# Attention's PSUM copies issued one slot later, and a respaced softplus, in a state-space, attention and graph-experts kernel

## The chip, the cores and the metric

The kernel runs on one core of one Trainium2 chip. The metric is device time in microseconds (us) from start to end of one execution; for the kernel before it is the median of three runs. Beside these there is one profiled execution, from which every busy time, wait and instruction duration below is taken.

## The reference, cut to what matters

Layer 0 is a group norm and two selective state-space passes ("t" along the 96 steps of each sequence, "d" along the 32 variables). Layer 1 is additive attention over 3072 tokens of each of 4 batches, then a graph attention that gates four experts. The change touches the step size of the state-space pass and the attention.

```python
# layer 0, both passes
xc = silu(conv1d(x @ in_w_x) + conv_b)
dt, Bm, Cm = split(xc @ xproj_w)
dt = softplus(dt @ dt_w + dt_b)                 # the softplus that the change respaces
h  = exp(dt * A) * h + dt * Bm * xc             # scan over the sequence, 16 states
y  = (sum_s(h * Cm) + xc * D) * silu(z)
x  = x + y @ out_w
# layer 1, attention, t = tokens of a batch
q, k = t @ Wt, t @ Wx
e = tanh(q[:, None, :] + k[None, :, :] + bh) @ Wa + ba
t = t + softmax(e) @ t                          # values: the normalized tokens
# then the graph attention, the gates and the experts (gelu)
```

## The kernel before, in words

**Order.** ScalarE (ACT), VectorE (DVE), TensorE (PE) and GpSimd (POOL) run in the order in which the program issues. It is written out by hand as slots. `Attention.units` and layer 0's `run` are two generators that are advanced in turn. A slot is: attention's tanh; the first half of layer 0's jobs (decay exponentials and scans); attention's score products; the second half of layer 0's jobs (the front of the next block, inputs, outputs, gates, side products of experts); attention's next small step from the list `todo`; one step of side work (`beside`: keys, or the table of a finished part). DMAs are issued from SP.

**Layer 0.** A block is 384 tokens and takes 48 slots, in which four chunks of 128 channels pass through 16 states. In every three slots `back` computes four decays dA (`decays`, exponential on ScalarE into one of two PSUM banks), and scans them on VectorE a slot later (`scans`, L395). GpSimd multiplies and sums (L402 to L411). Beside it `front` prepares the next block: the convolution, and from slot 31 the step sizes. `step` makes one chunk's softplus as max(s, 0) + log(1 + u) with u = exp(-|s|): a product pt into the PSUM bank "pp" (one buffer, shared with px, pd, pz and po); on VectorE max (L300) and -|s| (L301); on ScalarE u (L308); on GpSimd 1+u (L312); on VectorE (1+u)-1-u (L316), a rounding remainder that GpSimd subtracts from dt (L320). One logarithm over all four chunks (L329) and two additions (L335) end it. Blocks called `lead`, whose fronts run before attention begins, use other engines for some of these.

**Attention.** One tanh (L802) of 128 x 3072 elements serves four query rows. Its output th has three buffers. Two slots later 16 products (`scores`, L778) fold it into the PSUM tile pe (one buffer). Eight slots make a unit of 32 rows; at its end `unit_tail` takes the negated row maximum nb on VectorE (L848) and the exponential pr on ScalarE (L855). Then come, one per slot from `todo`: `turn` of four pieces (transposes, L862, and their copy pT, L864), `turn` of two, `values` (48 products, L871), `kept` (copy pvs, L877). Four units make a tile, whose tail goes on: `factors` (L900 to L907), `factors2` (L912, L914), `factors3` (exponential), `spread` (GpSimd, L921), `together` (L926), `outputs` (L934 to L937). If steps are left when the next unit ends, they are all issued at once, ahead of the new exponential. All these products, and the side work's, use one PSUM bank ("pv").

**Late part.** When layer 0 has ended, the first half of each slot is edge-sorting work on VectorE, paced by an estimate of 1.9 us, and the second half early expert products, paced by `att.extra`, the estimated TensorE time of the next step.

What a step looked like: the products and the copy that reads them stand together.

```python
for i in range(i0, i1):
    nc.tensor.transpose(pt[:, (i - i0) * P:(i - i0 + 1) * P], pr[:, i * P:(i + 1) * P], self.ident)
nc.vector.tensor_copy(pT[:, i0:i1, :].rearrange("p i x -> p (i x)"), pt[:, :(i1 - i0) * P])
```

Of the kernel before, what the change touches and what calls it, by code (L numbers as in the profile page):

```python
# [26 lines left out]
P = 128  # L27
# [47 lines left out]
class Layer0:  # L75
# [96 lines left out]
    def front(self, blk, lead):  # L172
# [107 lines left out]
        def step(e, s_mm, s_out):  # L280
# [22 lines left out]
            @at(s_out + 1)  # L303
            def _():
                if lead:
                    nc.scalar.activation(ua(), ua(), AF.Exp, scale=-1.0)
                else:
                    nc.scalar.activation(ua(), ua(), AF.Exp, bias=self.wf["dtb"][:, e:e + 1])  # L308

            @at(s_out + 2)  # L310
            def _():
                nc.gpsimd.tensor_scalar(ub(), ua(), 1.0, None, ALU.add)  # L312

            @at(s_out + 3)
            def _():
                nc.vector.scalar_tensor_tensor(ua(), ub(), 1.0, ua(), ALU.subtract, ALU.subtract)  # L316

            @at(s_out + 5)
            def _():
                nc.gpsimd.tensor_tensor(dt(), dt(), ua(), ALU.subtract)  # L320

        step(0, 33, 33)
        step(1, 34, 35)
        step(2, 36, 36)
        step(3, 37, 37)

        @at(41)
        def _():
            nc.scalar.activation(v["ub"], v["ub"], AF.Ln)  # L329

        for e in range(0, EC, 2):
            @at(44 + e // 2)
            def _(e=e):
                dt = blk["dt"][:, e:e + 2, :]
                nc.vector.tensor_tensor(dt, dt, v["ub"][:, e:e + 2, :], ALU.add)  # L335
# [11 lines left out]
    def back(self, blk, then):  # L347
# [121 lines left out]
        for e in range(EC):  # L469
# [18 lines left out]
            put(12 * e + 1, skip(e))  # L488
            put(12 * e + 4, gate_product(e), 0 if blk["lead"] else 1)
            put(12 * e + 5, gate_tanh(e))  # L490
            put(12 * e + 6, gate_out(e))
            if blk["lead"]:
# [139 lines left out]
class Attention:  # L632
# [4 lines left out]
    def __init__(self, ctx, tc, ident, a, x1, x2, xn2T, tab_s, tab_a):  # L637
# [34 lines left out]
        self.extra, self.entry, self.col, self.asked, self.normed = 0.0, 0, 0, 0, 0  # L672

    def psum(self, name):
        return self.ps_v.tile([P, JB], F32, tag="pv", name=name)
# [90 lines left out]
    def units(self, side):  # L766
# [23 lines left out]
        i = 0  # L790
        while i < B * PER + LAG or todo:
            b, col = self.entry, self.col = divmod(i, PER)
            if b < B and "krep" not in self.state[b]:

                yield
                yield
                beside()
                continue
            if b < B:
# [3 lines left out]
                behind.append(th)  # L803
            yield
            busy = tail = None
            if behind and i >= LAG:
# [10 lines left out]
            if tail:  # L817

                for f in todo:
                    f()  # L820
                todo = tail()
            elif todo:
                busy = todo.pop(0)()

# [13 lines left out]
    def unit_tail(self, b, n, pe):  # L838
# [20 lines left out]
        def turn(i0, i1):  # L859
            pt, pr, pT = self.psum("ptw"), v["pr"], v["pT"]  # L860
            for i in range(i0, i1):
                nc.tensor.transpose(pt[:, (i - i0) * P:(i - i0 + 1) * P], pr[:, i * P:(i + 1) * P],  # L862
                                    self.ident)
            nc.vector.tensor_copy(pT[:, i0:i1, :].rearrange("p i x -> p (i x)"),  # L864
                                  pt[:, :(i1 - i0) * P])

        def values():
            pv, pT = self.psum("pv"), v["pT"]
            for i in range(NK):
                for q in range(NQT):  # L870
                    nc.tensor.matmul(pv[q * QU:(q + 1) * QU, :C + 1], pT[:, i, q * QU:(q + 1) * QU],  # L871
                                     s["xn"][:, q * NK + i, :], start=(i == 0), stop=(i == NK - 1))
            s["pv"] = pv
            return "pv"

        def kept():
            nc.vector.tensor_copy(pvs[:, u, :], s["pv"][:, :C + 1])  # L877

        first, second = (lambda: turn(0, 4)), (lambda: turn(4, NK))
        first.us, second.us, values.us = 0.7, 0.4, 2.9  # L880
        steps = [first, second, values, kept]
        if u == NU - 1:
            first, *rest = self.tile_tail(b, t, nb, pvs)
            steps = steps[:3] + [lambda: (kept(), first())[1]] + rest
        return weights

    def tile_tail(self, b, t, nb, pvs):
# [9 lines left out]

        def factors():
            nc.sync.dma_start(x, src)
            nc.vector.tensor_scalar(mx, nb, -1.0, self.ba, ALU.mult, ALU.add)  # L900
            g = self.wk.tile([NU, QU], F32, tag="g", name="g")
            g4 = self.wk.tile([NU, NQT, QU], F32, tag="g4", name="g4")
            pm = self.psum("pm")
            nc.tensor.transpose(pm[:NU, :P], mx, self.ident)
            nc.vector.tensor_reduce(g, pm[:NU, :P].rearrange("p (q r) -> p r q", q=NQT), AX.X,
                                    ALU.max)
            nc.vector.tensor_copy(g4, g.unsqueeze(1).to_broadcast([NU, NQT, QU]))  # L907
            s["g4"] = g4

        def factors2():  # L910
            pf = self.psum("pf")
            nc.tensor.transpose(pf[:, :NU], s["g4"].rearrange("p q r -> p (q r)"),  # L912
                                self.ident[:NU, :NU])
            nc.vector.tensor_tensor(f, mx, pf[:, :NU], ALU.subtract)  # L914

# [7 lines left out]
        def together():  # L923
            po = self.psum("po")
            for u in range(NU):
                nc.tensor.matmul(po[u * QU:(u + 1) * QU, :C + 1], sf[:, u, :], pvs[:, u, :],  # L926
                                 start=True, stop=True)
            s["po"] = po
            return "po"

        def outputs():
            po = s["po"]
            sm = self.wk.tile([P, 1], F32, tag="sm", name="sm", bufs=2)
# [4 lines left out]

        return [factors, factors2, factors3, spread, together, outputs]

# [1090 lines left out]
```

## Time and profile before

| what | us |
|---|---|
| median of 3 runs (15839.43 to 15862.44) | 15854.98 |
| the profiled execution | 15480.32 |
| its span, first to last instruction | 15478.4 |
| ScalarE busy | 12181.5 (79%) |
| TensorE busy | 11840.1 (76%) |
| VectorE busy | 11076.9 (72%) |
| GpSimd busy | 8984.7 (58%) |
| 3072 tanh L802, 2847 ns each | 8665.9 |
| 49152 score products L778 | 5108.5 |
| 4096 scans L395, 940 ns each | 3682.6 |

Busy is the time in which an engine executes. A wait is the idle time of an engine just before an instruction, put down to what released that instruction: "DVE pT L864 <- PE ptw L862: 1119.9, 468, 13.7" says that VectorE stood idle for 1119.9 us in 468 places, at most 13.7 us in one, before the copy of line 864, until the transposes of line 862 had ended. Engines work their instructions in order, so whatever stands behind such a copy waits with it. Lines of groups give count, then busy us and mean ns, then idle before. Of lines that a wait or group names, L300 to L335 are softplus, L778 to L937 attention, L378 to L464 the states of layer 0.

### The profile page before, as it was taken

The numbers are of one execution on the slowest core, as the hardware profiler recorded it, in microseconds if no ns is written. First come the engines' busy times: TensorE is split into PE (matmuls) and PEld (weight loads), VectorE is DVE, ScalarE is ACT, GpSimd is POOL, SyncE is SP. The second block draws the span as 40 slices with busy tenths as digits, with TensorE's granted clock in tenths as the row PEclk, the third lists the DMA queues.
The fourth block names the chain that finished last, engine by engine and source line by source line (L and its number), as shares of the span: only waits on it lengthen the run. The fifth ranks groups of instructions, "written<-read, shape, count | busy, mean of one in ns | idle before, by whom it ended". The sixth has DMA issues, their size and how long they took to land.

```text
span 15478.4 us, 224265 instructions
## 1 busy us (share of the span) xinstructions
PE 11840.1 (76%) x86496; PEld 5192.8 (34%) x86496; DVE 11076.9 (72%) x15711; ACT 12181.5 (79%) x9326; POOL 8984.7 (58%) x6586
## 2 busy tenths in 40 slices
PE   5666665777777777878888777888877878887897
PEld 2222222222222233333333333333333334443454
DVE  7888888777777887777777877577767783331368
ACT  3443334999999979999999899999998989998221
POOL 4565557777777767777777677577750000007663
PEclk8888886888888878889998888999988989998998
DMA  5666665444444444454444444355541000001224
GB/s 190 203 206 200 199 201 163 144 146 152 148 147 148 153 157 145 148 151 149 149 146 154 149 147 150 113 153 153 150 129 40 25 15 15 8 25 22 52 62 127
DMA packets 1197834, 1986.89 MB, mean 128 GB/s; under 512 B 411985, under 2 KB 645073, under 8 KB 1194321
## 3 DMA queue, kind: packets, MB, share of 16 engines
q1 hardware_dynamic: 1169104, 1967.10, 41.1%
q0 software_dynamic: 27648, 5.36, 0.9%
q8 instruction: 680, 11.14, 0.3%
q14 instruction: 402, 3.29, 0.1%
HBM read 1864.71 MB, written 107.35 MB: 127 GB/s over the span
## 4 chain that ended last, share of the span: by engine, by line
ACT 32%; PE 23%; DVE 19%; POOL 11%; issue 10%; DMA 4%; SPq 0%; DVEq 0%; POOLq 0%; ACTq 0%
ACT th L802 23%; PE pe L778 9%; DVE h L395 7%; POOL h L402 5%; ACT dA L378 5%; POOL gd L1009 3%; PE pv L871 2%; DVE dB L386 2%; DMA bB<-bc 2%; PE pa L1333 2%; PE po L1585 1%; ACT pr L855 1%; PE ph L1577 1%; PE ptw L862 1%; POOL uab L312 1%
## 5 line engine op out<-in xcount | busy, mean ns | idle before, releaser
L802 ACT ACTIVATE th<-krep,qsel 128x3072 f32<-128x3072 f32 x3072 | 8665.9, 2847 | 406.0 <-PE pe L778 389.2
L778 PE MATMUL pe<-th,wa_blk 128*32 128x384 f32 x49152 | 5108.5, 544 | 1634.9 <-ACT pr L855 1259.7
L402 POOL TENSOR_TENSOR h<-h,bC 128x768 f32<-128x768 f32 x2048 | 3782.9, 1847 | 2869.2 <-DVE h L395 2641.1
L395 DVE TENSOR_TENSOR_SCAN h<-dA,dB 128x384 f32<-128x384 f32 x4096 | 3682.6, 940 | 822.9 <-ACT dA L378 624.8
L778 PEld LDWEIGHTS pe<-th,wa_blk 128*32 128x32 f32 x49152 | 1470.4, 117 | 4272.4 <-issue 1946.2
L386 DVE TENSOR_TENSOR dB<-bB,dtu 128x768 f32<-128x768 f32 x2048 | 1946.0, 950 | 133.3 <-DMA bB<-bc 89.3
L378 ACT ACTIVATE dA<-dt,t_A 128x380 f32<-128x380 f32 x2048 | 1134.1, 572 | 991.1 <-DVE h L395 985.9
L378 ACT ACTIVATE dA<-dt,d_A 128x372 f32<-128x372 f32 x2048 | 1109.2, 563 | 672.4 <-DVE h L395 666.2
L421 PE MATMUL py<-h,ident 128*128 128x384 f32 x2176 | 992.4, 588 | 688.9 <-POOL h L402 687.7
L921 POOL TENSOR_SCALAR sf<-sel,f 128x32 f32<-128x32 f32 x384 | 153.2, 422 | 2321.1 <-ACT f L917 2321.0
L409 POOL TENSOR_TENSOR h<-h 128x768 f32<-128x768 f32 x752 | 1424.2, 1894 | 46.9
L864 DVE COPY pT<-ptw 128x512 f32<-128x512 f32 (+1 forms) x768 | 426.1, 555 | 1123.9 <-PE ptw L862 1123.0
L871 PE MATMUL pv<-xn,pT 128*32 128x257 f32 x18432 | 1095.2, 385 | 84.2 <-DVE pT L864 82.5
L421 PEld LDWEIGHTS py<-h,ident 128*128 128x128 f32 x2176 | 437.1, 219 | 1248.7 <-POOL h L402 1021.7
L410 POOL TENSOR_TENSOR h<-h 128x384 f32<-128x384 f32 x752 | 798.1, 1061 | 59.0
L411 POOL TENSOR_TENSOR y<-y,h 128x384 f32<-128x384 f32 x752 | 768.3, 1022 | 59.0
L871 PEld LDWEIGHTS pv<-xn,pT 128*32 128x32 f32 x18432 | 586.1, 111 | 634.0 <-DVE pT L864 146.6
L1286 POOL DMA_INDIRECT gs<-tab_s,si x432 | 504.7, 1168 | 265.2 <-issue 121.8
L316 DVE SCALAR_TENSOR_TENSOR uab<-uab 128x384 f32<-128x384 f32 x256 | 389.8, 1523 | 198.6 <-POOL uab L312 194.6
L1659 ACT ACTIVATE h<-ph,b 128x512 f32<-128x512 f32 x148 | 100.4, 687 | 533.3 <-PE ph L1577 533.1
L1009 POOL DMA_INDIRECT gd<-tab_a,di x432 | 428.3, 991 | 133.0 <-issue 133.0
L848 DVE TENSOR_REDUCE nb<-pe 128x1 f32<-128x768 f32 x384 | 362.1, 943 | 197.2 <-PE pe L778 197.0
(292 smaller groups left out, 15388.4 us busy)
## 6 DMA issues: line engine op xcount, KB each, us to landing
bB<-bc SPq DMA_DIRECT2D x2048, 384.0 KB
bC<-bc SPq DMA_DIRECT2D x2048, 384.0 KB
all<-kept SPq DMA_DIRECT2D x19, 2048.0 KB
x<-x SPq DMA_DIRECT2D x144, 256.0 KB
x<-x SPq DMA_DIRECT2D x192, 128.0 KB
xt<-xn2T SPq DMA_DIRECT2D x41, 512.0 KB
kept<-ko SPq DMA_DIRECT2D x39, 512.0 KB
qsel<-xn2T SPq DMA_DIRECT2D x75, 256.0 KB
```

Source lines behind the costliest of these rows:

```text
L378: nc.scalar.activation(inner(dA[:, :T]), inner(blk["dt"][:, e, :]), AF.Exp, scale=blk["w"]["A"][:, e, i + s:i + s + 1])
L386: nc.vector.tensor_tensor(dB, blk["bB"].pop(j), z["dtu"].unsqueeze(1).to_broadcast([P, SB, T]), ALU.mult)
L395: nc.vector.tensor_tensor_scan(h[:, s, :], z.pop(("dA", e, i + s))[:, :T], z["dB"][:, s, :], 0.0, ALU.mult, ALU.add)
L402: nc.gpsimd.tensor_tensor(h, h, blk["bC"].pop(j), ALU.mult)
L409: nc.gpsimd.tensor_tensor(h0, h0, h1, ALU.add)
L410: nc.gpsimd.tensor_tensor(h0[:, 0, :], h0[:, 0, :], h0[:, 1, :], ALU.add)
L411: nc.gpsimd.tensor_tensor(y[e], y[e], h0[:, 0, :], ALU.add)
L421: nc.tensor.matmul(z["py"], self.ident, h[:, s, :], start=(i == 0), stop=(i == DS - 1))
L778: nc.tensor.matmul(pe[q * QU:(q + 1) * QU, j, :KQ // 2], self.wa[:, k, :], th[:, c0:c0 + KQ // 2], start=(k == 0), stop=(k == NK - 1))
L802: nc.scalar.activation(th, s["krep"], AF.Tanh, bias=s["qsel"][:, col:col + 1])
L871: nc.tensor.matmul(pv[q * QU:(q + 1) * QU, :C + 1], pT[:, i, q * QU:(q + 1) * QU], s["xn"][:, q * NK + i, :], start=(i == 0), stop=(i == N ...
L1009: self.nc.gpsimd.indirect_dma_start(out=self.gd[:, q, c, :], out_offset=None, in_=self.tab_a[q].rearrange("p n f -> (p n) f"), in_offset=b ...
```

## The change

*Attention.* A list `later` holds functions that issue VectorE work. The steps `turn`, `values`, `factors`, `factors2` and `together` issue their TensorE products at once and put the copy, reduction or output that reads them into `later`; `units` empties it in the next slot, after the first half of layer 0's jobs and before the scores. `kept` is no step of its own any more; `maxima` (the load of x and the first part of `factors`) goes into `later` behind a tile's last values. A step made by `step` has an estimate `us`; `units` issues side work ahead of such a step, and none in the slot of a step marked `full` (`values`, `together`). Other steps run as before.

*Softplus of blocks that are not `lead`.* u goes into a PSUM tile of the bank "ex", which expert side work uses in other slots. 1+u moves from GpSimd to VectorE, next to the remainder. Products stand at slots 33, 35, 37, 39 and their readers a slot later (before: 33, 34, 36, 37 and 33, 35, 36, 37). The subtraction on GpSimd comes three slots after the reader instead of five, the logarithm at slot 43 instead of 41, the additions at 44 and 46 instead of 44 and 45. The last chunk's gate moves by one slot (product 41, tanh 42, result 43).

```diff
                 if lead:
                     nc.scalar.activation(ua(), ua(), AF.Exp, scale=-1.0)
                 else:
-                    nc.scalar.activation(ua(), ua(), AF.Exp, bias=self.wf["dtb"][:, e:e + 1])
+                    v["u"] = self.ps_x.tile([P, 512], F32, tag="ex", name="u")[:, :T]
+                    nc.scalar.activation(v["u"], ua(), AF.Exp, bias=self.wf["dtb"][:, e:e + 1])
 
             @at(s_out + 2)
             def _():
-                nc.gpsimd.tensor_scalar(ub(), ua(), 1.0, None, ALU.add)
-
-            @at(s_out + 3)
-            def _():
-                nc.vector.scalar_tensor_tensor(ua(), ub(), 1.0, ua(), ALU.subtract, ALU.subtract)
-
-            @at(s_out + 5)
+                if lead:
+                    nc.gpsimd.tensor_scalar(ub(), ua(), 1.0, None, ALU.add)
+                else:
+                    nc.vector.tensor_scalar(ub(), v["u"], 1.0, None, ALU.add)
+                    nc.vector.scalar_tensor_tensor(ua(), ub(), 1.0, v["u"], ALU.subtract,
+                                                   ALU.subtract)
...
+            @at(s_out + (5 if lead else 3))
             def _():
                 nc.gpsimd.tensor_tensor(dt(), dt(), ua(), ALU.subtract)
 
-        step(0, 33, 33)
-        step(1, 34, 35)
-        step(2, 36, 36)
-        step(3, 37, 37)
-
-        @at(41)
+        for e, (s_mm, s_out) in enumerate(((33, 33), (34, 35), (36, 36), (37, 37)) if lead else
+                                          ((33, 34), (35, 36), (37, 38), (39, 40))):
+            step(e, s_mm, s_out)
+
+        @at(41 if lead else 43)
         def _():
             nc.scalar.activation(v["ub"], v["ub"], AF.Ln)
 
         for e in range(0, EC, 2):
-            @at(44 + e // 2)
+            @at(44 + e // 2 * (1 if lead else 2))
...
-            put(12 * e + 4, gate_product(e), 0 if blk["lead"] else 1)
-            put(12 * e + 5, gate_tanh(e))
-            put(12 * e + 6, gate_out(e))
+            g = 12 * e + (5 if e == EC - 1 and not blk["lead"] else 4)
+            put(g, gate_product(e), 0 if blk["lead"] else 1)
+            put(g + 1, gate_tanh(e))
+            put(g + 2, gate_out(e))
...
                 behind.append(th)
             yield
+            late, self.later = self.later, []
+            for f in late:
+                f()
             busy = tail = None
...
                 todo = tail()
+            elif todo and hasattr(todo[0], "us"):
+                if not todo[0].full:
+                    beside()
+                todo.pop(0)()
+                busy = True
             elif todo:
-                busy = todo.pop(0)()
+                todo.pop(0)()
...
-            nc.vector.tensor_copy(pT[:, i0:i1, :].rearrange("p i x -> p (i x)"),
-                                  pt[:, :(i1 - i0) * P])
+            self.later.append(lambda: nc.vector.tensor_copy(
+                pT[:, i0:i1, :].rearrange("p i x -> p (i x)"), pt[:, :(i1 - i0) * P]))
...
-            s["pv"] = pv
-            return "pv"
-
-        def kept():
-            nc.vector.tensor_copy(pvs[:, u, :], s["pv"][:, :C + 1])
-
-        first, second = (lambda: turn(0, 4)), (lambda: turn(4, NK))
-        first.us, second.us, values.us = 0.7, 0.4, 2.9
-        steps = [first, second, values, kept]
+            self.later.append(lambda: nc.vector.tensor_copy(pvs[:, u, :], pv[:, :C + 1]))
+
+        steps = [self.step(lambda: turn(0, 4), 0.7), self.step(lambda: turn(4, NK), 0.4),
+                 self.step(values, 2.9, True)]
         if u == NU - 1:
             first, *rest = self.tile_tail(b, t, nb, pvs)
-            steps = steps[:3] + [lambda: (kept(), first())[1]] + rest
+            steps[2] = self.step(lambda: (values(), self.later.append(first)), 2.9, True)
+            steps += rest
...
+            def late():
+                nc.vector.tensor_reduce(g, pm[:NU, :P].rearrange("p (q r) -> p r q", q=NQT), AX.X,
+                                        ALU.max)
+                nc.vector.tensor_copy(g4, g.unsqueeze(1).to_broadcast([NU, NQT, QU]))
+
+            self.later.append(late)
...
-            nc.vector.tensor_tensor(f, mx, pf[:, :NU], ALU.subtract)
+            self.later.append(lambda: nc.vector.tensor_tensor(f, mx, pf[:, :NU], ALU.subtract))
...
-            s["po"] = po
-            return "po"
-
-        def outputs():
-            po = s["po"]
+            self.later.append(lambda: outputs(po))
+
+        def outputs(po):
...
-        return [factors, factors2, factors3, spread, together, outputs]
+        return [maxima, self.step(factors, 0.2), self.step(factors2, 0.1), factors3, spread,
+                self.step(together, 1.5, True)]
```

More of the change, by code (lines that the diff above doesn't have):

```diff
@@ L307, in _ @@
                 else:
-                    nc.scalar.activation(ua(), ua(), AF.Exp, bias=self.wf["dtb"][:, e:e + 1])
+                    v["u"] = self.ps_x.tile([P, 512], F32, tag="ex", name="u")[:, :T]
+                    nc.scalar.activation(v["u"], ua(), AF.Exp, bias=self.wf["dtb"][:, e:e + 1])
             @at(s_out + 2)
             def _():
-                nc.gpsimd.tensor_scalar(ub(), ua(), 1.0, None, ALU.add)
-            @at(s_out + 3)
-            def _():
-                nc.vector.scalar_tensor_tensor(ua(), ub(), 1.0, ua(), ALU.subtract, ALU.subtract)
-            @at(s_out + 5)
+                if lead:
[4 more added lines that the diff above has]
+                                                   ALU.subtract)
+            if lead:
+                @at(s_out + 3)
+                def _():
+                    nc.vector.scalar_tensor_tensor(ua(), ub(), 1.0, ua(), ALU.subtract,
+                                                   ALU.subtract)
+            @at(s_out + (5 if lead else 3))
             def _():
                 nc.gpsimd.tensor_tensor(dt(), dt(), ua(), ALU.subtract)
-        step(0, 33, 33)
-        step(1, 34, 35)
-        step(2, 36, 36)
-        step(3, 37, 37)
-        @at(41)
+        for e, (s_mm, s_out) in enumerate(((33, 33), (34, 35), (36, 36), (37, 37)) if lead else
+                                          ((33, 34), (35, 36), (37, 38), (39, 40))):
+            step(e, s_mm, s_out)
+        @at(41 if lead else 43)
         def _():
@@ L672, in __init__ @@
         self.extra, self.entry, self.col, self.asked, self.normed = 0.0, 0, 0, 0, 0
+        self.later = []
     def psum(self, name):
@@ L790, in units @@
         i = 0
-        while i < B * PER + LAG or todo:
+        while i < B * PER + LAG or todo or self.later:
             b, col = self.entry, self.col = divmod(i, PER)
@@ L804, in units @@
             yield
+            late, self.later = self.later, []
+            for f in late:
+                f()
             busy = tail = None
@@ L872, in values, with step @@
                                      s["xn"][:, q * NK + i, :], start=(i == 0), stop=(i == NK - 1))
-            s["pv"] = pv
-            return "pv"
-        def kept():
-            nc.vector.tensor_copy(pvs[:, u, :], s["pv"][:, :C + 1])
-        first, second = (lambda: turn(0, 4)), (lambda: turn(4, NK))
-        first.us, second.us, values.us = 0.7, 0.4, 2.9
-        steps = [first, second, values, kept]
+            self.later.append(lambda: nc.vector.tensor_copy(pvs[:, u, :], pv[:, :C + 1]))
+        steps = [self.step(lambda: turn(0, 4), 0.7), self.step(lambda: turn(4, NK), 0.4),
+                 self.step(values, 2.9, True)]
         if u == NU - 1:
             first, *rest = self.tile_tail(b, t, nb, pvs)
-            steps = steps[:3] + [lambda: (kept(), first())[1]] + rest
-        return weights
+            steps[2] = self.step(lambda: (values(), self.later.append(first)), 2.9, True)
+            steps += rest
+        return weights
+    @staticmethod
+    def step(f, us, full=False):
+        g = lambda: f()
+        g.us, g.full = us, full
+        return g
     def tile_tail(self, b, t, nb, pvs):
@@ L896, in tile_tail, with maxima, factors @@
         src = self.x1[b].rearrange("v s c -> (v s) c")[t * P:(t + 1) * P, :]
-        def factors():
+        def maxima():
             nc.sync.dma_start(x, src)
             nc.vector.tensor_scalar(mx, nb, -1.0, self.ba, ALU.mult, ALU.add)
+        def factors():
             g = self.wk.tile([NU, QU], F32, tag="g", name="g")
@@ L904, in factors @@
             nc.tensor.transpose(pm[:NU, :P], mx, self.ident)
-            nc.vector.tensor_reduce(g, pm[:NU, :P].rearrange("p (q r) -> p r q", q=NQT), AX.X,
-                                    ALU.max)
-            nc.vector.tensor_copy(g4, g.unsqueeze(1).to_broadcast([NU, NQT, QU]))
             s["g4"] = g4
+            def late():
[3 more added lines that the diff above has]
+            self.later.append(late)
         def factors2():
```

## The prediction

> **What bounds the kernel now.** First the page's forty slices (busy tenths):
>
> ```profile
> PE   5666665777777777878888777888877878887897
> ...
> DVE  7888888777777887777777877577767783331368
> ACT  3443334999999979999999899999998989998221
> ```
>
> ScalarE is at nine tenths in almost every slice from 7 to 35, while attention's tanh runs (first 2568.3 us, last start 14349.5). The lead-in before and the tail after hold next to nothing that the change edits. So next comes the busy time of that stretch, cut where layer 0 ends; after start:end and length the columns are TensorE, its weight loads, VectorE, ScalarE, GpSimd:
>
> ```profile
> 2571.00:11450.00 8879.00, 6943.35 (x56800) 2869.83 (x56800) 6754.38 (x9209) 8370.86 (x6244) 6478.40 (x4635) 0.88 0.48 148
> 11450.00:14355.00 2905.00, 2345.59 (x23252) 1049.77 (x23256) 1493.37 (x2573) 2601.23 (x1086) 401.28 (x461) 0.91 0.09 25
> ```
>
> ScalarE works 10972 of 11784 us. Its work stays, so its idle time, 812 us or 5.2% of the span, caps the gain. The view of waits for ScalarE in this stretch says what ends it:
>
> ```profile
> ACT th L802 <- PE pe L778: 389.2, 346, 24.2
> ACT dA L378 <- DVE h L395: 303.3, 357, 7.4
> ACT pr L855 <- DVE nb L848: 97.4, 61, 14.2
> ```
>
> Tanh waits for a th buffer that the scores must release; the decay exponentials wait for a dA bank that a scan must release; the weights wait for the row maximum. Two of the three come from a late VectorE, which is only 76% busy before 11450. Why it is late stands in its own waits:
>
> ```profile
> DVE pT L864 <- PE ptw L862: 1119.9, 468, 13.7
> DVE h L395 <- ACT dA L378: 621.3, 380, 9.2
> DVE pvs L877 <- PE pv L871: 241.9, 112, 4.6
> ...
> DVE dt L300 <- PE pt L284: 151.3, 48, 5.1
> DVE sm L934 <- PE po L926: 118.2, 41, 30.1
> DVE g L905 <- PE pm L904: 99.1, 95, 3.7
> DVE uab L316 <- POOL uab L312: 91.9, 57, 3.0
> ...
> DVE f L914 <- PE pf L912: 68.1, 41, 5.5
> ```
>
> All but the second are VectorE standing at an instruction whose input TensorE or GpSimd has only just been asked for. The timeline shows what stands behind it (start, us, instruction, idle before it):
>
> ```profile
> 4128.79 0.69 DVE L864 COPY pT<-ptw 128x512 f32<-128x512 f32 x1 [2.38 <-PE ptw L862]
> 4129.40 1.80 DVE L395 TENSOR_TENSOR_SCAN h<-dA,dB 128x384 f32<-128x384 f32 x2
> ...
> 4133.42 0.43 DVE L864 COPY pT<-ptw 128x256 f32<-128x256 f32 x1 [1.23 <-PE ptw L862]
> 4133.76 1.80 DVE L395 TENSOR_TENSOR_SCAN h<-dA,dB 128x384 f32<-128x384 f32 x2
> ...
> 4139.58 0.62 DVE L300 TENSOR_SCALAR dt<-pt,d_dtb 128x384 f32<-128x384 f32 x1 [2.73 <-PE pt L284]
> ```
>
> Twice the scans queue behind a copy that waits for transposes, then behind softplus. The chain of waits from 4125.21 to 4139.58 lies on TensorE without a break (scores, transposes, scores, values, pt) and then passes to VectorE and the scans. So after each unit's weights TensorE, catching up, paces VectorE, and VectorE paces ScalarE: a loop of three engines. Last, the prices of softplus on VectorE, by group for 2571 to 11450, and the spread of L316 over the run (min/median/max ns):
>
> ```profile
> L316 DVE SCALAR_TENSOR_TENSOR uab<-uab 128x384 f32<-128x384 f32 x180 | 294.5, 1637 | 95.9 <-POOL uab L312 91.9
> ...
> L301 DVE SCALAR_TENSOR_TENSOR uab<-dt,pt 128x384 f32<-128x384 f32 x180 | 99.7, 554 | 6.2
> ...
> L300 DVE TENSOR_SCALAR dt<-pt,d_dtb 128x384 f32<-128x384 f32 x96 | 58.3, 607 | 78.7 <-PE pt L284 76.1 <-PE pf L912 2.5
> ```
> ```profile
> L316 DVE SCALAR_TENSOR_TENSOR uab<-uab x256: 525/1917/2221, 94.9 to 11291.6; 128x384 f32<-128x384 f32 x128
> ```
>
> The same operation on as many elements takes 554 ns with one operand in PSUM, and 1637 on average with both in SBUF.
>
> **What the Trainium skill says.** (1) "TensorE: Matmul & The Clock Gate", "Architectural detail": VectorE's and ScalarE's queues are strict first-in first-out. The timeline agrees: ready scans stand behind the copy. (2) "SBUF — State Buffer", "SBUF: two separate sides": VectorE with two SBUF inputs and GpSimd reading SBUF contend for one pair of ports, locked for a whole instruction. L316's 525 against 1917 ns is what that looks like. (3) "ScalarE: Activation LUTs", "Step-by-step": writing PSUM is quicker for ScalarE than writing SBUF. L378 into PSUM takes 560 ns for 372 elements, L308 into SBUF 600 for 384, so agreement is slight.
>
> **The change, part by part.** The sum is made in ScalarE's idle time, inside the profiled span of 15478.4 us (15480.3 with what lies around it). The median of the runs shown, 15854.98, is 2.4% longer and no view says why; I carry the gain over in proportion.
>
> *Copies a slot late (pT, pvs, g, f, outputs).* Counts and durations stay; 1647 us of VectorE's waits (1119.9+241.9+118.2+99.1+68.1) lose their cause, since each copy now comes after the next slot's scans. In turn TensorE gets the copies later, by at most two scans, 1.8 us. Behind a late first copy stand the second transposes (one PSUM bank serves all), behind the second the 48 products of values (2.8 us), behind these the next scores, and for them the tanh. The cover is the slot's own scores (1.5 us) and layer 0's products. Side work is issued ahead of the transposes instead of behind them: the bank changes hands as often. On SP the load of x and the store to x2 move with their steps, past some bB/bC fetches; waits on those fetches are 89 us in the whole run, so I cost that at nothing, 20 us at worst.
>
> *Softplus.* There are 184 chunks (46 fronts of 4). Per chunk VectorE loses an L316 of 1637 ns and gets two operations with a PSUM source; taking L300 and L301 as nearest rows, 607+554. That is 184 × 0.476 = 88 us less busy. If both took 525 (the fastest L316) it would be 108; if the port conflict stayed on the subtraction, 112 us more. I take 88. The 92 us waiting for GpSimd go, and most of the 151 for pt, since each product now has a slot of its own before its reader; TensorE's wait for that bank (90 us, pt after L301) goes too. GpSimd loses 184 × 1.24 = 228 us, worth nothing on the path: it waits 2095 us for scans anyway between 2700 and 11600. ScalarE gains 184 × 0.03 = 5 us and pays one more table load, 1.3 us. The logarithm moves from slot 41 to 43 and the first addition stays at 44, so VectorE can meet it unfinished: 1.28+1.49 us from load to end, mostly hidden by the two scans; at most 46 × 1 us of VectorE time. The last gate moves a slot with its bank: nothing.
>
> *What this does to ScalarE's idle time.*
> - dA waiting for scans, where both stages run steadily: 62.8 (2571–5400) + 73.7 (5800–8400) + 34.7 (9000–11450) = 171. Of VectorE's waits there other than for dA, about four fifths are removed, but some lateness is plain work: I take 70%, −120.
> - The same at the changes of batch (5400–5800: 84.4, 8400–9000: 47.7): VectorE is 84% and 81% busy, with keys' copies, which are not deferred. A quarter, −35.
> - Tanh waiting for scores before 11450, 166 us: the relief on pt against later values. Nothing, between −80 and +100.
> - The same after 11450, 223 us: the edge sort no longer stands behind copies, but TensorE is itself 81% busy. −35.
> - Weights waiting for nb, 97 us, 72 of them after 11450 behind the sort: −40.
> - ScalarE's own work: −4.
>
> Sum −234 us, 1.5% of the span; in proportion −240 on the median: 15615. What is late next is TensorE: tanh waiting for scores becomes the largest idle time, some 350 us.
>
> **The rivals.**
> - *The loop opens wholly.* With VectorE early, row maxima come at once, TensorE starts its scores earlier and tanh's waits halve too: −260 (dA) −190 (tanh) −70 (nb) = −520, taken at four fifths, −420: 15435. For it: the chain runs through all three engines. Against: TensorE is 78 to 81% busy and still loses 1260 us waiting for pr, which nothing here shortens.
> - *The waits only change names.* VectorE already waits 621 us for dA; being earlier it may just wait longer there, with ScalarE's idle moments set by bursts of true work. Gain 40: 15815. The form that the softplus part does not do what it says (the conflict stays) ends here too.
> - *TensorE turns late, slower.* In two slots of three the copy stands behind two scans. If 276 units lose the 1.8 us in two thirds of cases (331) and the 57 units beside the sort 1.9 us of sort each (108), 439 less the 234 is +205: 16060. It decides once TensorE reaches the second transposes or the values before VectorE has ended its scans, that is, when it has less than a slot's scores in front of it. For it: three th buffers leave TensorE about one slot. Against: after pr TensorE is behind; in 4125–4139 it came to each copy after what it would now wait for.
>
> **How the numbers follow.** Likeliest 0.58, at 15615, its own range 15485 to 15745 (gains of 110 to 370). Loop wholly open 0.15; names change 0.14; slower 0.13. The range for 8 in 10 runs from 15400, which takes in the open loop, to 15860, which takes in the changed names and leaves out the slower case. What a measurement of this kernel can tell from no change is about 0.2%, 32 us. Faster by more: 0.58+0.15+half of 0.14 = 0.80; the other half, 0.07, within it; slower 0.13.
>
> **What would show it.** The copy of pT should have hardly any idle time before it, and scans should wait longer for dA than 621 us. dA's wait for scans should fall from 303 to about 150, nb's from 97 to under 60, tanh's stay between 310 and 490. The subtraction should take about 550 ns and the new addition about 600. The prediction is wrong if tanh's wait for scores passes 600 us (the slower case), or if dA's wait stays above 250 with the copies' waits gone.

## The result, and the profile after

| kernel | median us | range | ratio to before |
|---|---|---|---|
| before (4 runs) | 15857.42 | 15839.43 to 15862.44 | |
| changed (4 runs) | 15725.33 | 15722.62 to 15731.67 | 0.9918 [0.9905, 0.9932] |

The change gains 132 us, 0.8%: the sign forecast, 55% of the size (240), and near the lower end of the likeliest range (gains of 110 to 370). Most of it comes out of the stretch with layer 0.

First a trap. The profiled execution of before, which the prediction worked in, spans 15478.4 us; all timed runs of before in this study lie between 15838 and 15877. A second profile of the same kernel, called "before, again" below, spans 15862.2 and is representative. The stages of both, and of the changed kernel (start of an event, us):

| event | before, first profile | before, again | changed |
|---|---|---|---|
| first tanh | 2568.3 | 2563.9 | 2555.4 |
| last scan of layer 0 | 11495.4 | 11491.5 | 11371.3 |
| edge sort done (copy of the edge counts) | 13914.1 | 13907.3 | 13779.5 |
| last tanh | 14349.5 | 14677.7 | 14529.6 |
| end of the span | 15478.4 | 15862.2 | 15723.6 |

The two executions of before agree within 7 us until the sort is done; then one takes 435 us to the last tanh and the other 770. So the first profile is sound up to there, and later comparisons use "before, again". Against it the changed kernel gains 8 us ahead of the first tanh, 112 with layer 0 (8927.6 to 8815.9), 8 to the end of the sort, 20 to the last tanh, and loses 10 in the tail: 138.6 us of span.

ScalarE in the page's forty slices of the changed kernel (busy tenths):

```profile
ACT  3444335999999989999998999999979899944121
```

ScalarE is at nine tenths up to slice 35 and then at four in two slices, which the first profile of before, with eight and nine there, does not have. That is the 770-us stretch; the page of before, again, shows it as well:

```profile
ACT  3443336999999979999998999999979899935121
```

Next ScalarE's waits from the first tanh to the end of the sort, before, again (us in all, times, longest):

```profile
ACT th L802 <- PE pe L778: 314.4, 318, 8.2
ACT dA L378 <- DVE h L395: 302.1, 358, 7.4
ACT pr L855 <- DVE nb L848: 96.5, 62, 13.8
```

and the same view of the changed kernel:

```profile
ACT th L815 <- PE pe L788: 315.5, 353, 8.0
ACT dA L385 <- DVE h L402: 154.8, 164, 7.4
ACT pr L876 <- DVE nb L869: 90.6, 46, 13.9
ACT f L947 <- DVE f L944: 28.5, 23, 3.5
```

The decay exponentials' wait for scans halves, by 147 us. Nothing else of weight is gained, and a wait that before did not have stands in the last line: the exponential of f. Together these waits fall from 713.0 to 589.4 us, by 124; and the stretch itself gets 119 us shorter (11343.4 to 11224.1). ScalarE's busy time in the whole run falls from 12183.1 to 12166.4, 17 more. The two make 141, against 139 of the span: the idle time outside this stretch changes by next to nothing.

VectorE's waits in the stretch with layer 0, before, again:

```profile
DVE h L395 <- ACT dA L378: 615.2, 377, 9.2
DVE pT L864 <- PE ptw L862: 603.1, 295, 11.7
DVE dt L300 <- PE pt L284: 153.1, 48, 5.1
DVE uab L316 <- POOL uab L312: 91.1, 58, 3.0
...
DVE pvs L877 <- PE pv L871: 45.4, 44, 3.5
```

and of the changed kernel:

```profile
DVE h L402 <- ACT dA L385: 713.8, 425, 8.8
DVE pT L885 <- PE ptw L883: 383.3, 194, 5.4
DVE pvs L894 <- PE pv L892: 317.1, 142, 4.6
...
DVE dt L342 <- ACT uab L336: 41.3, 30, 5.1
```

The waits of softplus for pt and for GpSimd are gone and those for f and g small, but the copies' waits are not: pT keeps 383 of 603 us, and pvs, the copy of the values, rose from 45 to 317. The pair went from 648 to 700.

Beside the sort, from the last scan of layer 0 to the edge counts, the waits change names outright. Before, again:

```profile
DVE pT L864 <- PE ptw L862: 417.6, 143, 13.7
DVE ol L1174 <- PE pc L1188: 177.7, 108, 4.2
DVE pvs L877 <- PE pv L871: 141.1, 52, 4.6
```

and the changed kernel:

```profile
DVE ol L1203 <- PE pc L1217: 370.3, 174, 12.8
DVE pvs L894 <- PE pv L892: 206.2, 88, 3.9
DVE pT L885 <- PE ptw L883: 162.3, 54, 11.7
```

ol is a table that the sort builds on VectorE; it waits for a buffer that the sort's own products pc must release. The three add up to 736 us before and 739 after.

### The profile page after: what moved, and what is told of

Its sections match the earlier page's. It is cut to its first block, busy times and chain, and to the rows that moved or that the text cites. A ratio compares the mean times of both kernels' runs of the same rounds, so it can differ in the third digit from the quotient of the medians.

```text
span 15723.6 us, 224219 instructions
## 1 busy us (share of the span) xinstructions
PE 11790.3 (75%) x86496; PEld 5153.3 (33%) x86496; DVE 10988.1 (70%) x15895; ACT 12166.4 (77%) x9327; POOL 8711.6 (55%) x6402
## 4 chain that ended last, share of the span: by engine, by line
PE 20%; ACT 16%; DVE 7%; issue 6%; DMA 1%; another core or an unknown queue 1%; POOL 1%; SPq 0%; DVEq 0%; ACTq 0%; POOLq 0%
ACT th L815 12%; PE pe L788 7%; PE pv L892 3%; ACT dA L385 2%; PE pa L1362 2%; PE po L1614 2%; PE ph L1606 2%; DVE h L402 1%; ACT pr L876 1%; PE ptw L883 1%; PE pc L1217 0%; PE pz L459 0%; DVE dB L393 0%; PE ex L1531 0%
## 5 line engine op out<-in xcount | busy, mean ns | idle before, releaser
L788 PE MATMUL pe<-th,wa_blk 128*32 128x384 f32 x49152 | 5053.8, 539 | 1635.2 <-ACT pr L876 1400.9
L393 DVE TENSOR_TENSOR dB<-bB,dtu 128x768 f32<-128x768 f32 x2048 | 1940.8, 948 | 117.9 <-DMA bB<-bc 85.2
L892 PE MATMUL pv<-xn,pT 128*32 128x257 f32 x18432 | 1159.4, 390 | 441.7 <-issue 311.9
L894 DVE COPY pvs<-pv 128x257 f32<-128x257 f32 x384 | 160.3, 418 | 827.5 <-PE pv L892 730.7
L883 PE MATMUL ptw<-ident,pr 128*128 128x128 f32 x2304 | 479.1, 326 | 111.3 <-DVE pT L885 45.5
```

Source lines behind the costliest of these rows:

```text
L393: nc.vector.tensor_tensor(dB, blk["bB"].pop(j), z["dtu"].unsqueeze(1).to_broadcast([P, SB, T]), ALU.mult)
L788: nc.tensor.matmul(pe[q * QU:(q + 1) * QU, j, :KQ // 2], self.wa[:, k, :], th[:, c0:c0 + KQ // 2], start=(k == 0), stop=(k == NK - 1))
```

## The experiments

Four readings stood against each other. *Both parts share the gain*, and the rest of the forecast was lost to waits that changed names. *Softplus alone* does it, by taking VectorE off the ports that it shares with GpSimd. *The placing is wrong*: the copies come too early or too late, and a better half slot gives the missing 100 us. *The late stretch hides it*: what swells to 770 us after the sort is a matter of its own. In the diffs "..." marks what is left out. Ratios are to before, measured on the same chip at the same time, with 95% intervals.

### Before once more

No edit: a second profile of the kernel before.

> The kernel before, profiled once more. Theory G: its first profile (span 15478) was an unusual execution, and the timed runs (15857) lose some 375 us while GpSimd issues the gathers of line 1009 and TensorE waits for issue, as the changed kernel's profile shows between 13780 and 14530. Then this profile again has the last of L1196 (the edge count) near 13914 and the last tanh at 14600 to 14750, with TensorE's waits for issue over 200 us in between. Rival T: the 375 us are spread evenly (a lower clock); then the edge count ends near 14250 and the last tanh follows some 440 us later. If the span is again near 15478, this run says nothing on either.

15864.24 us. Its stages and waits are those shown above. The first profile's 15478 us was an exception, so a part of what the prediction read (71 of the 223 us of tanh's waits after 11450 lie behind the sort) comes from a stretch that usually looks different. There TensorE waits 258.9 us at the values for nothing that the profile shows, as was expected.

### Each part alone

The attention part of the diff alone, on the kernel before:

> The changed kernel with the softplus of before: only attention's copies are deferred. If VectorE's head of queue at the transposes' copies was what held the scans (the prediction's first part), this alone gives most of the 132 us: -80 to -110, with dA's wait for scans near 200 us. If softplus was the main part, it gives under 40. If the deferral makes TensorE late, it is slower than before.

The softplus part alone:

> The kernel before with the respaced softplus alone. If the two parts add up, -25 to -50 us against before; dA's wait for scans falls from 303 to about 260, VectorE's waits for pt and for GpSimd's 1+u go, and the transposes' copies still cost some 1100 us of VectorE's idle time. Rival: worth 80 or more, since it frees 88 us of VectorE and 240 us of its waits.

Attention alone 15803.66 us, 0.9958 [0.9941, 0.9974], 66 us; softplus alone 15819.96, 0.9970 [0.9959, 0.9982], 50 us. They add up to 115 of the 132, so within what can be told neither needs the other. Attention alone fell short of its 80 to 110; softplus alone is at the upper end of its range. ScalarE's wait for scans is 201.9 us with attention alone and 226.4 with softplus alone, from 302: both act where the prediction put them (for softplus alone about 260 had been expected). The waits of softplus alone also show a cost, ScalarE's wait for nb:

```profile
ACT th L810 <- PE pe L786: 318.6, 341, 8.1
ACT dA L385 <- DVE h L402: 226.4, 265, 7.4
ACT pr L863 <- DVE nb L856: 145.6, 47, 16.7
```

It is 49 us longer than before, and with attention alone it is 28 us shorter (68.2). So of the forecast's −40 the attention part alone brings 28, and the softplus part works against it; the two don't simply add, since together they give −6. All of the 49 arises in the stretch with layer 0 (23.4 to 71.4), and there VectorE itself waits longer at nb for the scores, 93.7 us instead of 34.1. So there the row maximum in its turn waits for TensorE. Why softplus makes the scores late there was not tried.

### Softplus with u in SBUF

The changed kernel, but ScalarE writes u over its input in SBUF; 1+u and the remainder stay on VectorE in their new slots:

```diff
-                    v["u"] = self.ps_x.tile([P, 512], F32, tag="ex", name="u")[:, :T]
+                    v["u"] = ua()
```

> The changed kernel with u in SBUF again, 1+u still on VectorE. Port theory: the subtraction L317 takes 1.2 to 1.9 us instead of 0.55, and the time rises by 20 to 60 us. Rival: what matters in the softplus part is that the waits for pt and for GpSimd went; then within 15 us of 15725.

15794.03 us, 0.9958 [0.9943, 0.9973]: the ratio of attention alone, and some 63 us more than the changed kernel (20 to 60 were expected). ScalarE's wait for scans, 198.5 us, is that of attention alone as well (201.9). The groups of VectorE in the stretch with layer 0 (count, busy us, mean ns, idle before), the changed kernel:

```profile
L342 DVE TENSOR_TENSOR dt<-dt,uab 128x768 f32<-128x768 f32 x90 | 150.5, 1672 | 41.8 <-ACT uab L336 41.3
L317 DVE SCALAR_TENSOR_TENSOR uab<-uab,u 128x384 f32<-128x384 f32 x180 | 99.6, 554 | 6.2
L316 DVE TENSOR_SCALAR uab<-u 128x384 f32<-128x384 f32 x180 | 98.4, 547 | 6.1 <-ACT u L309 6.0
```

and with u in SBUF:

```profile
L317 DVE SCALAR_TENSOR_TENSOR uab<-uab 128x384 f32<-128x384 f32 x180 | 244.7, 1359 | 6.2
...
L316 DVE TENSOR_SCALAR uab<-uab 128x384 f32<-128x384 f32 x180 | 153.5, 853 | 4.6 <-ACT uab L309 4.5
```

The same two operations on the same elements cost 198.0 us with u in PSUM and 398.2 with it in SBUF. So the operand in PSUM carries what softplus brings: without it, the move of 1+u off GpSimd and the wider spacing of the slots bring nothing on balance. The two alone may still be worth something that their price on VectorE (398.2 us, where before spent 294.5 on L316) eats up; that was not taken apart. The Trainium skill, "SBUF — State Buffer", "SBUF: two separate sides", says that VectorE (with two SBUF inputs against a GpSimd that reads SBUF, or in a two-port mode) and GpSimd take one pair of ports for a whole instruction. This run agrees for L317, which has two SBUF inputs here: by the trace's records, of its 184 executions 137 start while a GpSimd instruction runs and take 1626 ns on average, and the 47 others take 557 to 561. With u in PSUM it takes 553 to 556 whatever GpSimd does. L316 has one SBUF input and behaves likewise: 1008 ns on average beside GpSimd (141 times, at most 2045), 327 to 360 alone (43 times). Whether it runs in a two-port mode no view shows. With u in PSUM it takes 524 to 558, slower than its best from SBUF and far quicker than its mean.

### The two waits that are new

The exponential of f in the slot of `spread`, one later, so that its input has been subtracted a slot ahead:

```diff
         def spread():
+            factors3()
             for u in range(NU):
...
-        return [maxima, self.step(factors, 0.2), self.step(factors2, 0.1), factors3, spread,
+        return [maxima, self.step(factors, 0.2), self.step(factors2, 0.1), lambda: None, spread,
```

> The changed kernel with a tile's exponential of f one slot later, in the slot of its spread. ScalarE's new wait f after f (28.5 us in 23 places) goes. If that wait is a loss by itself, -20 to -30 us against the changed kernel. Rival: the spread on GpSimd comes later, TensorE waits longer for sf (86 us in the stretch with layer 0) and passes it on; then within 10 us or slower.

The first addition after the logarithm at slot 45 instead of 44:

```diff
-            @at(44 + e // 2 * (1 if lead else 2))
+            @at(44 + e // 2 if lead else 45 + e // 2)
```

> The changed kernel with softplus's first addition at slot 45 instead of 44, so that it stands two slots behind the logarithm. VectorE's wait dt after uab (41 us in 30 places) goes. Theory: it is hidden in VectorE's slack, so 0 to -12 us. Rival: it delays scans and row maxima; then -20 to -40.

15712.54 us, 0.9911 [0.9896, 0.9926], and 15730.38, 0.9919 [0.9905, 0.9932]: neither differs from the change. In the first the 28.5-us wait for f is gone, and tanh's wait for scores is 341.0 us instead of 315.5: the wait changed its name. The second makes the additions quicker (1502 ns instead of 1672) and takes VectorE's wait for the logarithm away (41 us to 5.7), without effect on the time.

### The half slot in which a copy lands

Reading the issue order again shows why pvs waits: before, `kept` was a step of its own, in the second half of the slot after the values; the change flushes it at the end of the first half, half a slot *earlier*. (The copy pT stood in the second half of the slot of its transposes; the change moves it half a slot later, into the first half of the next.) A second list restores the old place for pvs and for the maxima behind it:

```diff
             yield
+            mid, self.mid = self.mid, []
+            for f in mid:
+                f()
             if tail:
...
-            self.later.append(lambda: nc.vector.tensor_copy(pvs[:, u, :], pv[:, :C + 1]))
+            self.mid.append(lambda: nc.vector.tensor_copy(pvs[:, u, :], pv[:, :C + 1]))
```

> The changed kernel with the copy pvs (and a tile's first maxima behind it) issued in the next slot's second half, where before had it, instead of the next slot's first half. VectorE's wait at pvs rose from 45 to 317 us in the stretch with layer 0; if that early place is what holds VectorE, the wait falls under 100, ScalarE's wait for scans (155 us) falls towards 120, and the time by 20 to 50 us against the changed kernel (15675 to 15705). Rival: the wait only moves to the next instruction, or TensorE waits for the later bank (its transposes pm after mx, 88 us before); then within 15 us of 15725, or slower.

15702.85 us, 0.9903 [0.9888, 0.9918]. VectorE's wait at pvs falls from 317 to 97 us and ScalarE's for scans to 122.7, but its wait for nb rises to 118.0. A gain of 23 us over the change would be at the edge of what can be told; the intervals overlap. So no more than that hangs on the early place of pvs, although 220 us of VectorE's waits do.

The next run keeps this and sends pT the same way too, half a slot later than the change has it:

```diff
-            self.later.append(lambda: nc.vector.tensor_copy(
+            self.mid.append(lambda: nc.vector.tensor_copy(
                 pT[:, i0:i1, :].rearrange("p i x -> p (i x)"), pt[:, :(i1 - i0) * P]))
```

> The changed kernel with the copies pT and pvs in the next slot's second half (pvs as in after_pvsmid). It asks where the price of a late copy begins. If TensorE has room, VectorE's wait at pT falls from 383 to under 150 us, ScalarE's wait for scans from 123 (after_pvsmid) to about 90, and the time is 20 to 40 us under after_pvsmid's 0.9903 of before (0.988). If TensorE has none, its wait for pT rises from 105 to over 250 us, tanh's wait for scores from 324 to over 400, and the time is that of the changed kernel or more.

15953.86 us, 1.0061 [1.0048, 1.0075]: slower than before. ScalarE's waits from the first tanh to the end of the sort:

```profile
ACT th L818 <- PE pe L788: 561.0, 466, 7.3
ACT dA L385 <- DVE h L402: 117.0, 110, 7.4
ACT pr L882 <- DVE nb L875: 100.0, 45, 14.0
```

and TensorE's in the stretch with layer 0, the changed kernel first:

```profile
PE pv L892 <- DVE pT L885: 104.8, 99, 4.1
...
PE ptw L883 <- DVE pT L885: 24.4, 19, 3.8
```

and this run:

```profile
PE pe L788 <- ACT pr L882: 1085.5, 260, 11.1
PE pv L898 <- DVE pT L891: 299.9, 159, 6.0
...
PE ptw L889 <- DVE pT L891: 114.5, 79, 5.8
```

VectorE now hardly waits at pT (56.3 us, from 383.3), and ScalarE waits less for scans than in the changed kernel (117.0 against 154.8). But VectorE's wait at pvs is back (297.0 us, from 96.8 in the run before this one), TensorE waits 414 us for the copy instead of 129, and tanh, behind TensorE, 245 us more. This is the prediction's slower rival with its own mechanism, half a slot beyond where the change stops. Of the places tried for pT, the change's is the latest that TensorE bears: the 383 us that VectorE still stands there can't be had by going half a slot further.

### The gathers behind the sort

Once the sort has written the indices and its scratch is free, the program issues 324 small gathers from GpSimd, three per slot. Windows across this stretch of the changed kernel (start:end, length, then TensorE, its weight loads, VectorE, ScalarE, GpSimd, granted clock, DMA share, GB/s):

```profile
14000.00:14100.00 100.00, 34.91 (x156) 10.83 (x160) 2.08 (x3) 15.73 (x7) 53.03 (x56) 0.56 0.06 7
14100.00:14200.00 100.00, 70.86 (x652) 28.21 (x644) 15.67 (x29) 76.46 (x31) 27.86 (x32) 0.90 0.08 15
14200.00:14300.00 100.00, 24.25 (x53) 5.30 (x53) 0.42 (x1) 4.44 (x3) 64.93 (x69) 0.50 0.07 2
14300.00:14400.00 100.00, 82.22 (x756) 38.93 (x755) 21.87 (x53) 91.02 (x39) 6.72 (x10) 0.91 0.10 30
```

Where GpSimd is at gathers for 53 to 65 of 100 us, TensorE gets through 156 and 53 products and ScalarE through a few tanh; where it pauses, 652 and 756. The gathers run in four bursts (75, 96, 96 and 57), and each time TensorE regains its pace 6 to 11 us after the last gather of the burst has started. The timeline shows how TensorE stands (start, us, instruction, idle before it):

```profile
13851.00 0.59 PE L892 MATMUL pv<-xn,pT 128*32 128x257 f32 x1 [2.21 <-issue]
13851.35 0.94 POOL L1038 DMA_INDIRECT gd<-tab_a,di  x1 [0.30 <-issue]
13852.40 0.12 PEld L892 LDWEIGHTS pv<-xn,pT 128*32 128x32 f32 x1 [2.67 <-issue]
13852.59 0.94 POOL L1038 DMA_INDIRECT gd<-tab_a,di  x1 [0.30 <-issue]
13853.80 0.59 PE L892 MATMUL pv<-xn,pT 128*32 128x257 f32 x1 [2.21 <-issue]
```

One product each 2.8 us, and before it a wait for "issue", that is for nothing that the profile shows; the same 48 products take 2.8 us together elsewhere. Over the stretch TensorE's waits of this kind at the values, and ScalarE's at tanh, which the view puts down to "remote" (another core or an unknown queue), add to:

```profile
PE pv L892 <- issue: 311.9, 92, 36.5
...
ACT th L815 <- remote: 298.6, 8, 52.5
```

In the first profile of before they are absent, with GpSimd gathering as closely, all 324 in one unbroken run:

```profile
14000.00:14100.00 100.00, 76.80 (x724) 34.08 (x720) 14.98 (x29) 79.11 (x32) 76.04 (x84) 0.86 0.17 21
```

So close gathers don't always bring the stall; that they bring it can be tested by spreading them. In the next runs gd is two tiles, so that half of it can be placed before the sort's scratch is given up, and gathers start when their indices are written (12597 us instead of 13780), at most one per slot. So that GpSimd doesn't run ahead, it copies one column of nb in each unit:

```diff
+        if self.pace is not None:
+            nc.gpsimd.tensor_copy(self.pace, nb[:, u:u + 1])
...
-                    for _ in range(3 if columns else 0):
+                    if columns is None and ed.listed and att.normed == B - 1:
+                        columns = [(q, c) for q in range(B - 1) for c in range(CQ)]
+                        att.pace = keep.tile([P, 1], F32, tag="pace", name="pace")
+                    if columns and columns[0][0] // 2 < len(ed.gds):
                         ed.gather(*columns.pop(0))
```

On the changed kernel:

> The changed kernel with the 324 early gathers of tab_a issued one per slot from the slot in which their indices are written (some 1170 us earlier), each unit's held back by a one-column GpSimd copy of that unit's row maximum, instead of three per slot after the edge count. Theory G: TensorE's and ScalarE's waits for issue while GpSimd gathers (312 and 299 us in the changed kernel's profile) shrink to a third or less, so -150 to -330 us against the changed kernel, 15400 to 15575. Rival: each gather takes its toll wherever it stands; then the waits for issue move forward with the gathers and the time stays within 60 us of 15725.

15490.24 us, 0.9757 [0.9741, 0.9773]. From the end of the sort to the last tanh it takes 381 us instead of 750, and "issue" before the values is 6.3 us instead of 311.9. Against that the sort ends 139 us later (13918.8): where gathers run beside it, tanh waits 126.1 us for scores and 29.3 more at "remote", against 42.6 in the changed kernel over the same part.

On the kernel before:

> The kernel before with the early gathers paced as in after_paced. If what the gathers cost has nothing to do with the change, it gains the same 235 us, so about 15625, 0.9852 of before, and the change is worth some 130 us on top of it (after_paced 0.9757). Rival: in the paced kernel the change is worth less or more by over 40 us.

15601.37 us, 0.9837 [0.9822, 0.9852]. With the stretch relieved, the change is worth 0.9757 / 0.9837 = 0.9919 (each against its own runs of before), the same as without: the two are independent, and the missing 100 us of the forecast are not hidden there. The paced gathers gain 250 us on before, a little more than the 235 expected.

The paced kernel with the late exponential and the later pvs:

> The changed kernel with the paced gathers, pvs in the next slot's second half and the exponential of f with its spread. If the three add up: 0.9757 less 0.0015 less 0.0007, 0.9735 of before, about 15440. Rival: with the gathers paced TensorE binds the late part, and the two small ones give nothing; then 0.9757.

15478.57 us, 0.9759 [0.9746, 0.9773]: no better than paced alone, so the two small moves are dropped.

Last, one gather in every second slot:

```diff
+                    slot += 1
-                    if columns and columns[0][0] // 2 < len(ed.gds):
+                    if columns and slot % 2 and columns[0][0] // 2 < len(ed.gds):
```

> after_paced with one gather in every second slot instead of in every slot (those not done by the end of attention are issued in the tail). In after_paced the stretch from the first gather to the edge count became some 130 us longer for 216 gathers, 0.6 us each. If the toll is of each gather, the time stays at 0.9757 of before within 0.2%, or is longer because more of them fall into the tail. If it is of their crowding, the time falls by another 40 to 100 us, to 0.970 to 0.973.

15341.41 us (15331.89 to 15389.33), 0.9678 [0.9662, 0.9695], the fastest of all. The toll ahead of the sort's end is gone as well: it ends at 13790.3, and tanh waits 42.1 us for scores from the first gather to there. One window from the sort's end to the last tanh:

```profile
13790.00:14136.00 346.00, 295.60 (x2835) 125.81 (x2832) 69.34 (x137) 335.96 (x140) 60.27 (x82) 0.96 0.12 34
```

The changed kernel spends 337.76 us of ScalarE's work in 750 us there; this one the same work in 346. The gain over one per slot, some 125 us by the ratios, is more than the 40 to 100 expected. Not all is free: 70 of the 324 gathers fall behind the last tanh, and that tail takes 1251 us in this profile (1194 in the changed kernel). The profiled execution, 15389.33 us, is the slowest of the four, so how much of this the others pay is open. This run and the paced changed kernel differ in the spacing alone; what the earlier start is worth by itself was not tried.

## Why the prediction was right, and where it was not

- *What bounds the kernel.* Right up to the end of the sort: ScalarE with a loop through VectorE and TensorE. The profile was taken as typical although it was 2.4% below the median, "and no view says why". The difference lies in a stage the prediction never opened, 770 us instead of 435 of span. It did not hurt the sum much, since the change is worth the same 0.8% with and without it.
- *dA waiting for scans, −155.* It measured −147, by both parts together. The step that carried the forecast was right in size, but its reason only in part: it rested on four fifths of VectorE's waits other than for dA being removed, and VectorE's idle time of that kind in the stretch with layer 0 fell only from 1529 to 1401 us. The scans became earlier because the waits now stand behind them, not because they went; that the size fits is partly luck.
- *Tanh waiting for scores, 0 before 11450 and −35 after.* It measured +11 and −10 up to the end of the sort. The term supposed that the sort would no longer stand behind copies. What it no longer waits at pT came back elsewhere: VectorE's three waits there are 736 and 739 us, and the sort waits 193 us longer for its own products (370.3, from 177.7). Behind the sort, where TensorE stalls beside the gathers, ScalarE's idle time did not fall at all (408 and 412 us).
- *Weights waiting for nb, −40.* It measured −6: +17 with layer 0, −23 after. The softplus part works against what the attention part takes off. With the line above this is the mis-sized part of the sum: −75 forecast, −5 measured over the two.
- *What was left out.* The exponential of f, 28.5 us: the change puts the subtraction behind the next slot's scans and leaves the exponential in that very slot. The prediction costed the deferral for TensorE alone and did not ask which ScalarE instruction reads f. Mending it gave no time, so this is a symptom of the loop rather than a price of its own.
- *"1647 us of VectorE's waits … lose their cause".* This step failed. It treated pT, pvs, g, f and outputs as moved alike, a slot later. g and f moved behind the next slot's scans and lost most of their waits (79.8 to 15.8 and 36.7 to 14.6 us); pT moved just as far and kept 64% of its wait; pvs moved half a slot earlier and took on 272 us. On TensorE a wait of 67.6 us for g is new. For this the rival *the waits only change names* was partly right: scans wait for dA 99 us longer, as the prediction said they would, and pvs holds the rest.
- *"At most two scans, 1.8 us" later for TensorE.* Sound at the change's place: TensorE's wait for pT rose only from 67 to 105 us. The *slower* rival was real, but begins half a slot further (1.0061).
- *Softplus, 88 us less of VectorE.* Its two operations measured 547 and 554 ns, 98 us less than L316 had taken (296.1 in before, again; 198.0). VectorE as a whole fell from 11074.8 to 10988.1, 87 us, so the sum came out right, but terms that nobody had priced in part cancel in it: in the stretch with layer 0 the two additions grew from 1198 to 1672 ns (43 us) and the small copy of g from 556 to 1370 (55 us), while the operations that write dtu and xc took 57 us less. The wait of the first addition for the logarithm was bounded at 46 us and measured 41. TensorE's wait for the bank of pt, which was to go, did not: 87.9 before, 94.5 after.
- *ScalarE's own work, −4.* It measured −17. The exponential of u fell from 600 to 566 ns. That agrees with the Trainium skill, "ScalarE: Activation LUTs", "Step-by-step", by which ScalarE writes PSUM quicker than SBUF, but it is only 6 us. The decay exponentials, which the change does not touch, took 12 us less (2243.1 to 2230.9); why is open.
- *SP's queue, nothing.* Right: VectorE's wait for bB is 85.2 us against 86.3.

Left open: what holds TensorE and ScalarE up while gathers run close together, and why the first profiled execution was spared. The DMA queues have room (a share of 0.06 to 0.10 in the windows above). Instructions, too, come by DMA queues (the page lists 680 and 401 such packets), but a wait for such a packet does not explain the end of a stall: after each of the four bursts TensorE regained its pace before the next of these packets started (by 14079 us, for instance, and the packet at 14088.8). The end of the gathers is what precedes it. Which part of softplus delays the scores, and so nb, was not tried either.

## What to carry to other kernels

When copies are issued later, settle for each one the half slot in which it lands and where it stood before, and list every reader on every engine; here one of the "later" copies came earlier, and another half slot of delay turned a gain of 0.8% into a loss of 0.6%. Compare the profiled execution's time with the timed median before building a sum on it, and where they differ open every stage. Background gathers can be worth spreading thin, as here, even where their engine and the DMA queues look idle; look at the tail too, into which some of them then move.

## What had not been expected of the hardware

- Beside 324 gathers of 0.94 us each, 0.30 us apart, a stretch lasted 750 us that another run passes in 346, with products at one per 2.8 us and the granted clock at 0.50 to 0.63 in the starved windows. One per slot cost about 0.6 us each on the path (from the first gather to the sort's end 1321.6 us instead of 1195.0, over 216 gathers); one per two slots, nothing up to the last tanh. In one execution the same gathers at the same distance cost nothing of the kind (435 us).
- The addition 1+u on VectorE (384 elements a partition) took 327 to 360 ns from SBUF while GpSimd stood still, and 1008 on average, up to 2045, when GpSimd was at work as it started; from PSUM 524 to 558 either way.
